# Tail chains in groups of three, and a last pooled attention with its keys in partitions

## The chip, the cores and the metric

The kernel runs on one core of a Trainium2 chip. The metric is device time in microseconds (us) for one execution, the median over runs on the chip.

## What is computed

Four images of 256 channels and 64 x 64 pixels pass through four layers. Each adds the group norm of its input, passed through the layer, to that input.

```python
x = x + layer0(gn(x))   # 1x1 conv, offsets and a gather of 9 points per group, 1x1 convs
x = x + layer1(gn(x))   # qkv (1x1), depthwise 5x5 on qkv, linear attention over both, 1x1 projection
x = x + layer2(gn(x))   # 3x3 conv with binarised weights
x = x + layer3(gn(x))   # pooled attention:
    theta = conv1x1(x); phi, g = conv1x1(maxpool2x2(x))
    m1 = softmax(theta^T phi, over the 1024 pooled keys)     # 4096 queries per image
    m4 = conv1x1(m1 g) + x
```

## The kernel before

All data is float32, with 128 channels on the partitions. The work of an image goes through `convolve` and `offsets`, then `sample` (the gather, `L596`, on GpSimd's queue), `feedforward`, `layer1`, `layer2`, `layer3`. A small planner, `beside`, lays generators side by side: each yields a cost after a piece of work, and is advanced in proportion to a share of the whole. While image n is gathered, the layers of images n-1 and n-2 are written in between. Inside `ordered()` the order of the program is the order of every engine's queue (PE, DVE, ACT, POOL); outside it a list scheduler of the compiler orders them. DMAs are issued by SP.

After the last gather three stages are left, and all that the diff touches and that runs differently lies there (`self.alone` is true):

1. *The tail* (`ordered`): `feedforward` of the last image, then its `layer1` beside `layer2` and most of `layer3` of the image before it. The planner is told that `layer1` costs `LAST` units.
2. `layer2` of the last image, beside the rest of that `layer3` (not ordered).
3. `layer3` of the last image, alone (`wide`, not ordered).

In `layer1`, `rows` makes q, k, v in blocks of 512 pixels and writes them with borders into `pad` tiles of 16 rows (`room(3)` gives four buffers here). 24 *chains* follow: 6 groups of 128 channels x 4 pieces of 16 rows, each a depthwise 5x5, that is 25 products and sums. `aggregate` does a chain on DVE with 25 instructions (the first `L180`, the others `L178`) that accumulate in PSUM (`agg`). `products` does one on ACT, which makes 25 products `m` (`L196`, `L198`), and POOL, which adds 24 of them (`L200`). Here 9 (`ASIDE`) of the 24 are done by `products`: the generator `others` takes the next chain whenever it has finished one, and `step` advances it by 0.67 pieces per DVE instruction through `due`.

What uses the results (transposes and copies `kt` for the sums over pixels, then `output`: `dens`, reciprocal, heads, projection) is put into a list `later` in small stages, and `step` takes one entry for every second DVE instruction. What is left in the list when the last chain has ended is run after it; this is called the drain below.

`layer2` loads each block with a border into `xp` (two buffers here), normalises it on ACT (`L1053`), makes four sums and differences `xd` on POOL (`L1041`), and multiplies (`L1090`).

`layer3` handles 128 queries at a time, 32 times per image, with queries on the partitions: two score matmuls of 512 keys (`L1190`, with the strided slice `tv[:, q]` of `th` as weights), two maxima (`L1191`), `Exp` with the maximum as bias (`L1196`), eight transposes by PE (`L1202`) with two copies `pT` (`L1204`), eight matmuls with `gt` (`L1208`), whose last column of ones gives the softmax's sum, a reciprocal and a scaling `m2` (`L1211`, `L1213`). After each four, a projection (`L1218`), the residual (`L1219`, `L1220`) and a store. For the last image the scores lie in turn in the banks `acc` and `dp` and in the two banks of `agg`. PSUM has eight banks: three `mm`, one `vk`, two `agg`, and `acc` and `dp`.

Of the kernel before, what the change touches and what calls it, by code (L numbers as in the profile page):

```python
# [38 lines left out]

CONVOLVE, OFFSETS, BINARY = NB * 9 + 26, 60, 62  # L40
FEED = NB * 40 + 8
LINEAR, LAST, ASIDE = 938, 592, 9
STEPS = 900
CONV, SECOND = NB * 22.5 + 11, 568
EPS_BN = 1e-5
# [26 lines left out]
class Net:  # L72
# [14 lines left out]

    def long(self):

        return self.ps1.tile([P, 512], F32, name="ps", tag=next(self.idle)) if self.alone else self.ps()  # L90

    def rsqrt(self, pool, v, eps, cols, name):

# [464 lines left out]
    def sample(self, n, ssum):  # L558
# [8 lines left out]
        def halves(name):  # L567

            t = self.ps1.tile([P, 2, 256], F32, name=name, tag=name)
            return cycle([t[:, 0], t[:, 1]])  # L570

        accs, dps = halves("acc"), halves("dp")

        def load(b):
            blocks[b] = sl = sp.tile([P, BR, G * 5], F32, name="sl")
# [181 lines left out]
    def layer1(self, n, st, st2):  # L757
# [3 lines left out]
        with tc.tile_pool(name=f"la{n}", bufs=1, side="right") as sp, \  # L761
# [10 lines left out]
            ld = sp.tile([P, 4, 2, 32], F32, name="ld")  # L772
            nc.vector.memset(ld, 0.0)

            later, count, aside, due = [], 0, None, 0
            alone = self.alone
            room = lambda bufs, more=1: bufs + more * alone

            def step(cost, chains=False):


                nonlocal count, due
                count += chains
                if later and (not alone or count % 2 or not chains):
                    later.pop(0)()
                if chains:
                    if count % 8 == 6 if alone else count in LEADS:
                        next(made, None)
                    if aside:
                        due += ASIDE * 28 / (6 * NCH - ASIDE) / 25  # L790
                        while due > 1:
                            next(aside, None)
                            due -= 1
                return cost


# [12 lines left out]
            def rows():  # L809


                for t, tiles in enumerate(((2, 4), (3, 5), (0, 1))):
                    new = lambda c: [self.padded(bp, 1, 20, 2, c, f"pad{i}", bufs=room(3)) for i in range(2)]
                    pads = {0: new(0)}
                    for b in range(NB):
                        c, h = divmod(b, 2)
# [36 lines left out]
            def products(pd, i, name, done, relu=True, **more):  # L853

                out = bp.tile([P, 16, W], F32, name=name, tag="av2", bufs=3)
                yield from self.products(bp, out, pd, self.w5[:, i], 5, 16, W, 0, self.b5[:, i:i + 1], lambda cost: cost)
                end(out, done, relu, **more)
# [149 lines left out]
                    yield step(3)  # L1007
                return args

            def others():  # L1010

                for _ in range(ASIDE):
                    while not (args := next(every)):
                        yield
                    *args, more = args
                    yield from products(*args, **more)

            if alone:
# [13 lines left out]
    def layer2(self, n, st, st3, side="left"):  # L1032
# [3 lines left out]
        with tc.tile_pool(name=f"ca{n}", bufs=1, side=side) as sp, \  # L1036
# [6 lines left out]
            def normed(b):  # L1043

                lo, hi = max(8 * b - 1, 0), min(8 * b + 9, H)
                xp = bp.tile([P, KT, 10, W + 2], F32, name="xp", bufs=1 + self.alone)
                for v in [xp[:, :, :, 0:1], xp[:, :, :, W + 1:]] + [xp[:, :, 0:1, 1:W + 1]] * (b == 0) \
                        + [xp[:, :, 9:10, 1:W + 1]] * (b == NB - 1):
                    nc.vector.memset(v, 0.0)
                for k in range(KT):  # L1050
                    v = xp[:, k, lo - 8 * b + 1:hi - 8 * b + 1, 1:W + 1]
                    nc.sync.dma_start(v, self.x4_d[n][:, k, lo * W:hi * W].rearrange("p (r w) -> p r w", w=W))
                    nc.scalar.activation(v, v, AF.Identity, bias=bi[:, k:k + 1], scale=sc[:, k:k + 1])  # L1053
                d = xp.rearrange("p k r (x d) -> p k r x d", d=2)
                return [d[:, :, :, c // 2:c // 2 + W // 2, c % 2] for c in range(4)]
# [49 lines left out]
    def layer3(self, n, st, wide=False):  # L1105
        nc, tc, a = self.nc, self.tc, self.a
        M = HW // 4
        with tc.tile_pool(name=f"na{n}", bufs=1, side="left") as sp, \
# [66 lines left out]


            tv = th.rearrange("p (n j) -> p j n", j=NT)
            for b in range(NB):
                m2 = bp.tile([P, 512], F32, name="m2")
                for j in range(4):  # L1180
                    if not wide and not self.spare:
                        s = [self.ps("s") for _ in range(2)]
                    elif wide and j % 2:
                        s = self.ps1.tile([P, 2, 512], F32, name="s", tag="agg")
                        s = [s[:, i] for i in range(2)]
                    else:
                        s = [self.ps1.tile([P, 512], F32, name="s", tag=tag) for tag in ("acc", "dp")]
                    mx = bp.tile([P, 3], F32, name="mx3")
                    for i in range(2):
                        nc.tensor.matmul(s[i], tv[:, 4 * b + j], ph[:, i * 512:(i + 1) * 512], start=True, stop=True)  # L1190
# [32 lines left out]
    def run(self):  # L1223
# [40 lines left out]
        with self.tc.tile_pool(name="gather", bufs=2, side="left") as self.gp, \  # L1264
# [124 lines left out]
```

## Time and profile before

| | us |
|---|---|
| median of 3 runs | 8705.34 (8691.91 to 8707.14) |
| profiled execution | 8769.03 |
| its span | 8767.3 |
| last gather's end, about | 7290 |
| `feedforward` of the last image, about | 7300 to 7520 |
| chains of the last `layer1` on DVE | 7551.6 to 8254.1 |
| drain of their uses | 8254.1 to 8358 |
| last `layer2`, first matmul to last store, about | 8380 to 8560 |
| last `layer3`, its queries' loop | 8590.4 to 8763.4 |

The profile is one execution, taken by the hardware. A group of instructions is given with its line, engine, operation, tiles, count, busy time and mean ns, then the idle time of the engine before them and what ended it. PE is the matmul engine, PEld its weight loads, which overlap with matmuls; a float32 matmul is two instructions. PEclk is the matmul clock that was granted, as a share of full speed.

### The profile page before, as it was taken

Reading aid. Unit: us, or ns where it says so; the run is one execution under the profiler, and the core shown is the slowest. Engines: PE = TensorE matmul, PEld = TensorE weight load, DVE = VectorE, ACT = ScalarE, POOL = GpSimd, SP = SyncE. Lnnn points to the kernel's source line nnn. Section 1 sums busy time; section 2 is a strip of 40 time slices with the busy share of each in tenths; the row PEclk is TensorE's granted clock in tenths of the full one; section 3 lists DMA queues with packets and bytes.
Section 4 is the critical chain, followed back from the end, with each engine's and each line's share of the span. In section 5 each row is a group of like instructions: output and inputs, shape, how many; then the busy total and the mean of one; then the engine's idle time right before and its main releaser. Section 6 shows DMA issues by size and latency. Waiting matters only on the chain.

```text
span 8767.3 us, 99783 instructions
## 1 busy us (share of the span) xinstructions
PE 5927.3 (68%) x35776; PEld 3524.6 (40%) x35776; DVE 4790.2 (55%) x6020; ACT 3564.8 (41%) x10792; POOL 4995.0 (57%) x4894
## 2 busy tenths in 40 slices
PE   4454554448744546688876676888766768987899
PEld 2222222223322322335644443345544433664476
DVE  5344442443366667324776675127766762588723
ACT  2333333234433433344444443444444442456414
POOL 2666666556666666666665556666655560487410
PEclk7666666669866667799987787999878879987899
DMA  6454554454433334444443344444433342220131
GB/s 171 129 157 123 144 150 117 119 146 142 153 107 108 105 109 125 135 130 141 135 133 106 110 115 141 141 133 139 139 105 109 111 118 95 77 68 30 44 96 53
DMA packets 744383, 1031.75 MB, mean 118 GB/s; under 512 B 354128, under 2 KB 459984, under 8 KB 742352
## 3 DMA queue, kind: packets, MB, share of 16 engines
q0 software_dynamic: 221184, 604.27, 24.1%
q1 hardware_dynamic: 522704, 421.10, 16.3%
q8 instruction: 283, 4.64, 0.2%
q14 instruction: 212, 1.74, 0.1%
HBM read 856.39 MB, written 168.61 MB: 117 GB/s over the span
## 4 chain that ended last, share of the span: by engine, by line
PE 42%; another core or an unknown queue 18%; DVE 16%; ACT 13%; issue 8%; POOL 2%; DMA 1%; SPq 0%; ACTq 0%; DVEq 0%; POOLq 0%
DVE agg L178 9%; PE acc L603 6%; PE ps L739 5%; ACT wm L588 5%; PE ps L1090 5%; PE ps L749 5%; PE ps L824 3%; PE ps L946 2%; PE ps L1208 2%; PE s L1190 2%; PE po L636 2%; ACT dT L623 2%; ACT at L608 1%; POOL av L200 1%
## 5 line engine op out<-in xcount | busy, mean ns | idle before, releaser
L596 POOL DMA_INDIRECT g<-tab,sl x4608 | 4401.8, 955 | 2848.3 <-issue 1184.1
L178 DVE SCALAR_TENSOR_TENSOR agg<-pad,vec,agg 128x1024 f32<-128x1024 f32 x2257 | 2904.0, 1287 | 63.3
L603 PE MATMUL acc<-g,wm 128*32 128x128 f32 x18432 | 1018.1, 339 | 2033.0 <-ACT at L608 1573.1
L603 PEld LDWEIGHTS acc<-g,wm 128*32 128x32 f32 x18432 | 562.9, 130 | 2532.2 <-ACT at L608 1785.6
L588 ACT ACTIVATE wm<-sl,con 128x48 f32<-128x48 f32 x6144 | 1486.9, 364 | 25.5 <-remote 12.0
L1090 PE MATMUL ps<-xd,w 128*128 128x256 f32 x3072 | 745.9, 395 | 28.6 <-issue 19.1
L623 ACT COPY dT<-dp 64x128 f32<-64x128 f32 x1152 | 296.3, 257 | 972.9 <-remote 475.5
L1090 PEld LDWEIGHTS ps<-xd,w 128*128 128x128 f32 x3072 | 594.4, 199 | 144.4 <-issue 61.1
L608 ACT COPY at<-acc 128x256 f32<-128x256 f32 x576 | 214.4, 372 | 774.5 <-remote 670.6
L739 PE MATMUL ps<-x2f,f 128*128 128x512 f32 x1024 | 506.6, 643 | 11.8 <-DVE hm L724 7.7
L824 PE MATMUL ps<-xr,qw 128*128 128x512 f32 x768 | 469.2, 741 | 19.5 <-issue 7.4
L724 DVE SCALAR_TENSOR_TENSOR hm<-ps,vec,lk 128x512 f32<-128x512 f32 x256 | 190.6, 749 | 518.7 <-ACT lk L741 391.6
L749 PE MATMUL ps<-hm,f 128*128 128x512 f32 x1024 | 463.5, 601 | 0.0
L200 POOL TENSOR_TENSOR av<-av,m 128x1024 f32<-128x1024 f32 x144 | 342.9, 2382 | 110.8 <-ACT m L196 102.0
L741 ACT ACTIVATE lk<-ps,low 128x512 f32<-128x512 f32 x256 | 174.3, 687 | 529.2 <-PE ps L739 401.5
L1041 POOL TENSOR_TENSOR xd<-xp 128x640 f32<-128x640 f32 x64 | 79.5, 1270 | 522.7 <-ACT xp L1053 421.9
L878 ACT COPY kt<-pt 128x512 f32<-128x512 f32 x256 | 149.2, 583 | 532.5 <-remote 255.6
L636 PE MATMUL po<-dT,ow 128*128 128x288 f32 x1024 | 328.7, 468 | 49.5 <-issue 14.1
L1208 PE MATMUL ps<-gt,pT 128*128 128x129 f32 x2048 | 316.8, 316 | 44.2 <-ACT pT L1204 34.8
L613 PE MATMUL dp<-ident,at 128*128 128x128 f32 x1152 | 288.2, 340 | 83.0 <-ACT dT L623 55.6
L1208 PEld LDWEIGHTS ps<-gt,pT 128*128 128x128 f32 x2048 | 299.1, 227 | 96.4 <-ACT pT L1204 45.8
L1190 PE MATMUL s<-ph,th 128*128 128x512 f32 x512 | 287.6, 673 | 46.0 <-ACT pad L836 12.6
(243 smaller groups left out, 7700.2 us busy)
## 6 DMA issues: line engine op xcount, KB each, us to landing
g<-tab,sl POOLq DMA_INDIRECT x4608
x<-x SPq DMA_DIRECT2D x128, 512.0 KB
xr<-x SPq DMA_DIRECT2D x96, 512.0 KB
tab<-xo SPq DMA_DIRECT2D x192, 128.0 KB
x<-in_x SPq DMA_DIRECT2D x32, 512.0 KB
y<-yc SPq DMA_DIRECT2D x32, 512.0 KB
yb<-y SPq DMA_DIRECT2D x64, 256.0 KB
x<-yb SPq DMA_DIRECT2D x64, 256.0 KB
```

The source lines that it names most:

```text
L178: nc.vector.scalar_tensor_tensor(to, s, wt, acc, ALU.mult, ALU.add)
L588: nc.scalar.activation(wm[:, :, :, o], blocks[b][:, r:r + WR, G:], AF.Copy, scale=self.con("own")[:, o:o + 1])
L596: nc.gpsimd.indirect_dma_start(out=g[:, i, :], out_offset=None, in_=table, in_offset=bass.IndirectOffsetOnAxis(ap=sl.bitcast(I32)[:, r, i: ...
L603: nc.tensor.matmul(acc[32 * i:32 * i + 32, :], wm[:, r4, 4 * i + 2 * x:4 * i + 2 * x + 2, :], g[:, i, x * P:(x + 1) * P], start=x == 0, st ...
L623: nc.scalar.copy(dT[b][hs, :, r:r + UR], dp[u][hs, :, :, s, :].rearrange("p v g o -> p g v o"))
L636: nc.tensor.matmul(po[m][:, 0:BR * OB], self.ow[:, k, m * P:(m + 1) * P], dT[b][:, k].rearrange("p r o -> p (r o)"), start=k == 0, stop=k ...
L739: nc.tensor.matmul(ps, f1[:, k, m * P:(m + 1) * P], x2[:, k], start=k == 0, stop=k == KT - 1)
L749: nc.tensor.matmul(ps, f2[:, k, m * P:(m + 1) * P], hm[:, k], start=k == 0, stop=k == 4 * KT - 1)
L824: nc.tensor.matmul(ps, qw[:, k, m * P:(m + 1) * P], x[:, k], start=k == 0, stop=k == KT - 1)
L1090: nc.tensor.matmul(ps[:, e], w[:, k, t, 2 * half + e, m * P:(m + 1) * P], v[:, 2 * half + e, k, t:t + 8], start=i % 6 == 0, stop=i % 6 == 5)
L1190: nc.tensor.matmul(s[i], tv[:, 4 * b + j], ph[:, i * 512:(i + 1) * 512], start=True, stop=True)
L1208: nc.tensor.matmul(ps[:, 0:P + 1], pT[:, m], gt[:, m], start=m == 0, stop=m == 7)
```

## The change

*Chains.* `ASIDE`, `others` and `due` go. Chains are taken in groups of three: the first and third on DVE, the second on ACT and POOL beside them, a piece for every second DVE instruction; what is left of the second is written at the group's end. So 8 chains are done by `products` and 16 by `aggregate`. `LAST` becomes 624. The second `pad` tile gets one more buffer, `xp` one fewer.

*PSUM.* The banks `acc` and `dp` become one tile `pair` of two banks, in `sample` and after it.

*Last `layer3`.* A new function `turned` makes the scores with keys on the partitions: eight matmuls of 128 keys x 128 queries, `ph` as weights and `tv[:, q]` as the moving operand. The maximum over the keys is taken in two steps, over the eight tiles in PSUM by DVE (with a step of 128 elements) and, after a transpose, over the partitions. To have it along the free axis, ACT spreads it over a 128x128 tile, PE multiplies that with the identity, ACT copies it to SBUF. DVE subtracts it from all 1024 scores of a partition; ACT takes `Exp` of all 1024 at once; the result is already in the form that the matmuls with `gt` need.

```diff
-LINEAR, LAST, ASIDE = 938, 592, 9
+LINEAR, LAST = 938, 624
...
-        return self.ps1.tile([P, 512], F32, name="ps", tag=next(self.idle)) if self.alone else self.ps()
+        return self.pair[:, next(self.idle)] if self.alone else self.ps()
...
-        accs, dps = halves("acc"), halves("dp")
+        pair = self.ps1.tile([P, 2, 2, 256], F32, name="pair", tag="pair")
+        accs, dps = (cycle([pair[:, i, 0], pair[:, i, 1]]) for i in range(2))
...
-                    if aside:
-                        due += ASIDE * 28 / (6 * NCH - ASIDE) / 25
-                        while due > 1:
-                            next(aside, None)
-                            due -= 1
+                    if count % 2 and aside:
+                        next(aside, None)
...
-                    new = lambda c: [self.padded(bp, 1, 20, 2, c, f"pad{i}", bufs=room(3)) for i in range(2)]
+                    new = lambda c: [self.padded(bp, 1, 20, 2, c, f"pad{i}", bufs=room(3) + (alone and i)) for i in range(2)]
...
-            def others():
-
-                for _ in range(ASIDE):
-                    while not (args := next(every)):
-                        yield
-                    *args, more = args
-                    yield from products(*args, **more)
-
-            if alone:
-                aside, number = others(), ASIDE
             while number < 6 * NCH:
                 count = 0 if not alone and number % 2 == 0 else count
                 *args, more = yield from chain()
-                yield from aggregate(*args, **more)
-                number += 1
-            if aside:
-                for _ in aside:
-                    pass
+                if alone:
+
+                    *slow, smore = yield from chain()
+                    aside = products(*slow, **smore)
+                    yield from aggregate(*args, **more)
+                    *args, more = yield from chain()
+                    yield from aggregate(*args, **more)
+                    for _ in aside:
+                        pass
+                    number += 3
+                else:
+                    yield from aggregate(*args, **more)
+                    number += 1
...
-                xp = bp.tile([P, KT, 10, W + 2], F32, name="xp", bufs=1 + self.alone)
+                xp = bp.tile([P, KT, 10, W + 2], F32, name="xp", bufs=1)
...
+            def turned(q, out):
+
+
+                if q % 2:
+                    s = self.ps1.tile([P, 8, P], F32, name="s", tag="agg")
+                else:
+                    s = self.pair.rearrange("p b (m q) -> p (b m) q", q=P)
+                for m in range(8):
+                    nc.tensor.matmul(s[:, m], ph[:, m * P:(m + 1) * P], tv[:, q], start=True, stop=True)
+                mk = bp.tile([P, P], F32, name="mk")
+                nc.vector.tensor_reduce(mk, s.rearrange("p m q -> p q m"), AX.X, ALU.max)
+                ps = self.ps()
+                nc.tensor.transpose(ps[:, 0:P], mk, self.ident)
+                mq = bp.tile([P, 1], F32, name="mq")
+                nc.vector.tensor_reduce(mq, ps[:, 0:P], AX.X, ALU.max)
+                mb = bp.tile([P, P], F32, name="mb")
+                nc.scalar.activation(mb, self.ones, AF.Copy, scale=mq)
+                nc.tensor.matmul(ps[:, P:2 * P], mb, self.ident, start=True, stop=True)
+                mr = bp.tile([P, P], F32, name="mr")
+                nc.scalar.copy(mr, ps[:, P:2 * P])
+                e = bp.tile([P, 8, P], F32, name="e", tag="pe")
+                nc.vector.tensor_tensor(e, s, mr.unsqueeze(1).to_broadcast([P, 8, P]), ALU.subtract)
+                nc.scalar.activation(e, e, AF.Exp)
+                pa = self.ps()
+                for m in range(8):
+                    nc.tensor.matmul(pa[:, 0:P + 1], e[:, m], gt[:, m], start=m == 0, stop=m == 7)
+                rden = bp.tile([P, 1], F32, name="rden")
+                nc.vector.reciprocal(rden, pa[:, P:P + 1])
+                nc.scalar.activation(out, pa[:, 0:P], AF.Copy, scale=rden)
...
+                    if wide:
+                        turned(4 * b + j, m2[:, j * P:(j + 1) * P])
+                        yield 9.5
+                        continue
+                    s = [self.pair[:, i] if self.spare else self.ps("s") for i in range(2)]
...
-        self.idle, self.alone, self.spare = cycle(["acc", "dp"]), True, True
+        self.pair = self.ps1.tile([P, 2, 512], F32, name="pair", tag="pair")
+        self.idle, self.alone, self.spare = cycle([0, 1]), True, True
```

More of the change, by code (lines that the diff above doesn't have):

```diff
@@ L565, in sample @@
         blocks, images, at, dp, dT, po, later = {}, {}, {}, {}, {}, {}, {}
-        def halves(name):
-            t = self.ps1.tile([P, 2, 256], F32, name=name, tag=name)
-            return cycle([t[:, 0], t[:, 1]])
-        accs, dps = halves("acc"), halves("dp")
+        pair = self.ps1.tile([P, 2, 2, 256], F32, name="pair", tag="pair")
+        accs, dps = (cycle([pair[:, i, 0], pair[:, i, 1]]) for i in range(2))
         def load(b):
@@ L773, in layer1 @@
             nc.vector.memset(ld, 0.0)
-            later, count, aside, due = [], 0, None, 0
+            later, count, aside = [], 0, None
             alone = self.alone
@@ L779, in step @@
             def step(cost, chains=False):
-                nonlocal count, due
+                nonlocal count
                 count += chains
@@ L1180, in layer3 @@
                 for j in range(4):
[L1181 to L1187, printed above, removed]
+                    if wide:
[3 more added lines that the diff above has]
+                    s = [self.pair[:, i] if self.spare else self.ps("s") for i in range(2)]
                     mx = bp.tile([P, 3], F32, name="mx3")
```

## The prediction

> **What bounds the kernel now.** I read the page first: the busy time of each engine and the forty slices.
>
> ```profile
> PE 5927.3 (68%) x35776; PEld 3524.6 (40%) x35776; DVE 4790.2 (55%) x6020; ACT 3564.8 (41%) x10792; POOL 4995.0 (57%) x4894
> ...
> PE   4454554448744546688876676888766768987899
> ...
> ```
>
> The whole-span shares say little, because the diff touches only what comes after the last gather, at 7290 us of 8767. So I asked for busy times by stretch: the tail's chains (first to last depthwise instruction on DVE), the drain of their uses, and the last pooled attention from its first score matmul to its last.
>
> ```profile
> 7551.60:8254.10 702.50, 563.45 (x2319) 391.00 (x2318) 630.62 (x714) 437.68 (x596) 545.53 (x242) 0.86 0.17 51
> 8254.10:8358.00 103.90, 92.97 (x321) 50.50 (x320) 42.96 (x68) 30.51 (x50) 0.00 (x0) 0.89 0.16 54
> ...
> 8590.40:8754.70 164.30, 159.15 (x886) 122.78 (x886) 64.79 (x139) 92.31 (x170) 0.00 (x0) 1.00 0.13 46
> ```
>
> The columns are length, then PE, PEld, DVE, ACT, POOL, the granted clock. Chains: DVE works 630.6 of 702.5 us, so DVE bounds them. Drain: PE works 93 of 104. Pooled attention: PE works 159.2 of 164.3, 97%, at full clock, and DVE and ACT have room. Next, the groups and DVE's waits in the chain stretch.
>
> ```profile
> L178 DVE SCALAR_TENSOR_TENSOR agg<-pad,vec,agg 128x1024 f32<-128x1024 f32 x345 | 443.3, 1285 | 8.3
> L200 POOL TENSOR_TENSOR av<-av,m 128x1024 f32<-128x1024 f32 x144 | 342.9, 2382 | 110.8 <-ACT m L196 102.0
> L196 ACT ACTIVATE m<-pad,vec 128x1024 f32<-128x1024 f32 x216 | 246.6, 1158 | 63.0 <-POOL av L200 43.7 <-POOL ak L200 19.0
> ```
>
> ```profile
> DVE rden L1211 <- PE ps L1208: 10.7, 5, 4.9
> ...
> DVE pad L459 <- ACT m L196: 9.2, 1, 9.2
> DVE r L1220 <- PE ps L1218: 4.2, 4, 1.9
> ...
> DVE g_mv L117 <- POOL av L200: 2.0, 1, 2.0
> ```
>
> Last, the groups of the pooled loop.
>
> ```profile
> L1190 PE MATMUL s<-ph,th 128*128 128x512 f32 x128 | 68.9, 638 | 4.2 <-DVE mx L1191 4.2
> L1208 PE MATMUL ps<-gt,pT 128*128 128x129 f32 x512 | 63.4, 276 | 0.5 <-ACT pT L1204 0.5
> L1208 PEld LDWEIGHTS ps<-gt,pT 128*128 128x128 f32 x512 | 61.8, 191 | 8.6 <-issue 4.3 <-ACT pT L1204 1.8
> L1191 DVE TENSOR_REDUCE mx<-s 128x1 f32<-128x512 f32 x64 | 44.3, 691 | 60.0 <-PE s L1190 59.6
> ...
> L1190 PEld LDWEIGHTS s<-ph,th 128*128 128x128 f32 x128 | 34.3, 303 | 12.7 <-DVE mx L1191 8.2 <-issue 0.5 <-ACT ph L1165 0.2
> ```
>
> A weight load of the strided `tv` takes 303 ns where one of packed `pT`, also 128x128, takes 191. This matters below.
>
> **The tail's chains.** Before, 9 of 24 chains run on ACT and POOL, 15 on DVE; after, 8 and 16. So DVE gets 25 more instructions. Five of them in a row took 6.58 us in the timeline, 1.315 us each: +33 us on the engine that bounds. POOL loses 24 adds of 2.38 us (57 us) and ACT 25 products of 1.16 us (29 us); neither bounds, so that by itself gives nothing. What it can give is less waiting on DVE. DVE's waits in the stretch, without the 15.3 us before its first chain, sum to 60 us. Two have a cause that the change takes away: the 9.2 us where the memset of a new `pad1` waits for a chain on ACT to finish with its buffer (`pad1` gets a fifth buffer and no such chain is behind any more), and the 2.0 us behind POOL. The waits behind PE (10.7 and 4.2 us shown) and 3.7 us behind ACT's `ph` could shrink if ACT waits less for POOL (63 us now): at most 18.6 us more. So the tail lies between 33-9.2-2.0-18.6 = +3 and, with nothing given back and a little lost, +38.
>
> The little is `xp` with one buffer. In the timeline an `xp` load is issued within 0.05 us of the end of POOL's adds on the block two before; with one buffer it will follow the adds of the block just before. The adds for block b+1 stand in the last quarter of block b; a block lasts some 35 us; the load takes 4 to 5 us (issue at 8383.66, ACT starts on it at 8387.48 and 8388.72); ACT's use stands an eighth of a block into the next. That is about even: 0 to 2 us a time on ACT, and `m`, `v` and `kt` are queued behind it, then POOL and PE. Seven blocks: 0 to 5 us for DVE, whose idle waits cover part. SP's queue holds the `xr` loads behind a waiting `xp`; these have a second buffer. In the last convolution a block takes 20.7 us against load 5, ACT 2 and POOL 5, so nothing there.
>
> The order of uses: counting the deferred uses through the code, 38 are left when the last chain ends before, 34 after; the `dens` and reciprocal (4.0 us of DVE) of the third output move ahead of that end, and some 5 us of PE leave the drain. Against that, linear's steps now sum to 613 of the 624 given, so about one query of the previous image's attention runs alone after it, 5 us of PE beside the last store. These cancel: drain 0, between -6 and +6. `pair` in place of `acc` and `dp` is the same two banks with the same readers: 0. For the tail I take +20, halfway, since the two waits with a named cause, 11 us, are all I can point at.
>
> **The last pooled attention.** Per query before: 164.3/32 = 5.13 us. PE after: scores 16 instructions of 128 columns, at the pace of L1208 (16 in 1.79 us in the chain) 1.8 us in place of 1.93; eight transposes (0.87 us) go and one (0.11) and a broadcast matmul (0.22) come; output matmuls 1.8 and projection 0.45 stay. That is 4.4 us against 5.05: if PE still bounded, -0.7 us each.
>
> But the path through one score buffer gets longer, and there are two buffers. Before, a buffer was free after scores, two maxima and `Exp`, and its next links needed no buffer. After, it is held for: scores 1.8; maximum over 1024 (0.69 for 512 plus 512 more at the same pace) 1.22; transpose with its load 0.45; maximum over 128 (as L1166) 0.29; `mb` (as L148) 0.40; broadcast matmul 0.5; `mr` (as L1213) 0.35; subtraction of 1024 (as L178) 1.29. Sum 6.3, with eight handoffs of about 0.1, 7.1 us. Two buffers give 3.55 us a query if no link ever waits for its engine. But each engine runs in order, and the other query is half a turn away: the small maximum stands behind a subtraction (1.29), the subtraction behind a maximum (1.22), `mb` behind an `Exp` of 1024 (1.05 as L861 to 1.24 as L198; 1.2), the broadcast behind the output matmuls (1.8). If each link loses that, 7.1+5.5 = 12.6 us a turn, 6.3 a query; if half, 4.9. I laid the instructions out in written order with these durations, each engine taking the earliest written one that is ready, and the two turns locked with the links behind the long ones; so I take the full loss.
>
> The other unknown is the scores' new moving operand, `tv[:, q]`, read with a step of 128 bytes. No matmul of the trace streams such a step; the nearest row is the weight load of the same tile, 112 ns longer than the packed one. Lower bound: no cost (1.8 us). Upper: the same 0.11 us on each of 16 instructions, 3.5 us. I take the upper, as it is the same data through the same engine. The turn is then 14.3 us, 7.15 a query, and PE's own work 6.1. [...] The maximum's read of PSUM with a step of 512 bytes is bounded likewise: 1.22 as above (the nearest, L274 with a step of 1 KB in SBUF, takes 1.04 us for 768) to 1.9 (L529, 288 elements written with gaps, 0.69 against 0.45); I take 1.22.
>
> Sum: 32 x (7.15-5.13) = +65, and the last query's drain is some 3 us longer: +68. With PE busy 85% of the time the clock may fall: 0.89 was granted in the drain at 89% busy, which would add 0.35 us a query, 11 us. Its gaps were up to 5 us and these would be about 1, so I take none and keep 11 for the range.
>
> The profiled execution took 8769.0 us around its span of 8767.3, 0.7% over the median of 8705.3; the differences are small, and I put them on the median unscaled: 8705+20+68 = 8793.
>
> **Rivals.**
> 1. *The step costs PE nothing, the turns still lock*: 32 x (6.3-5.13)+3 = +40, with the tail +20: 8765. [...] Against: the weight load.
> 2. *PE stays the bound* (the other side). In the pooled loop, if the links lose under 1.7 us a turn, PE's work without gaps, 4.4 us, sets the pace: 32 x (4.4-5.13)+3 = -20; with the tail at +3, 8688, and 8682 with the drain at its low end; I price it at 8685. It decides where a turn is under 8.8 us. For it: DVE needs 3.3 and ACT 2.7 us a query, both under 4.4. Against: 7.1 us of links alone.
> 3. *The change does nothing*: the tail's freed waits equal its extra chain and the pooled loop lands at 5.1: 8705.
>
> **How the numbers follow.** A measurement of this kernel tells about 0.2%, 17 us, from no change. Forecast 0.60, rival 1 0.21, rival 2 0.11, rival 3 0.08. The forecast and rival 1 are slower: 0.81; rival 2 faster 0.11; 0.08 same. The low end is rival 1 with the links losing most but not all of 5.5 us (5.5 a query, +15) and the tail at +15: 8735, taken down to 8718 to come near rival 3; rival 2 and most of rival 3, under 2 in 10, stay out. The high end is the forecast with the tail at +38, the clock's 11 and the slower maximum (0.68 a turn, 11): 8835.
>
> **What would show it.** DVE's depthwise instructions after the last gather 400 in place of 375, and the chain stretch some 20 us longer; POOL's idle up, its adds 192; no wait of `pad` for `m`. In the pooled loop PE busy about 85% instead of 97%, waits of the `mr` and subtraction links in front, score matmuls about 0.2 us apart. I am wrong if the loop's PE stays over 95%, or if the score instructions come 0.11 us apart, or if DVE's stretch does not grow.

## The result, and the profile after

The kernel after takes 8941.55 us (median of 5 runs, 8936.2 to 8957.21) against 8707.14 before (8691.91 to 8712.71): the ratio is 1.0272 with a 95% interval of 1.0260 to 1.0284, that is +234 us. The forecast was +88.

I cut both profiles at four points that can be found in any variant: the last matmul of the last `feedforward`, the end of the last depthwise instruction on DVE, the first matmul of the last `layer2`, and the first score matmul of the last `layer3`. Busy times by these stretches, for after (length, then PE, PEld, DVE, ACT, POOL with instruction counts, the granted clock, the DMA share and GB/s):

```profile
7462.10:8272.70 810.60, 606.24 (x2393) 395.11 (x2394) 669.58 (x794) 420.39 (x589) 495.28 (x224) 0.85 0.17 52
8272.70:8390.50 117.80, 101.03 (x362) 58.03 (x362) 43.10 (x87) 37.47 (x61) 1.74 (x2) 0.92 0.26 85
8390.50:8660.80 270.30, 220.40 (x940) 176.23 (x939) 64.41 (x151) 32.82 (x51) 37.79 (x31) 0.94 0.23 66
8660.80:8955.40 294.60, 233.19 (x1154) 208.18 (x1152) 98.92 (x145) 75.48 (x144) 0.00 (x0) 0.83 0.08 27
```

The same four stretches of before lasted 731.0, 126.0, 210.3 and 177.0 us. So three of them grew, by 80, 60 and 118 us, and the drain shrank by 8. The forecast had 20, 0, 68 and 0. DVE works 83% of the first stretch (669.6 of 810.6), and PE 79% of the last, with a clock of 0.83 where it had 1.00. (After's profiled run took 8957.2 us, 16 over its median. Before's was 62 over its median, but that lies ahead of the first cut, which came at 7523.0 against 7462.1 us. So the 249 us between the stretches' sums, less after's 16, agree with the 234 between the medians.)

What DVE waited for in the first stretch of after (total, times, longest), to be held against the waits in the prediction:

```profile
DVE mx L1210 <- PE pair L1209: 46.7, 31, 2.2
DVE x L1061 <- PE pair L1081: 26.2, 7, 17.2
DVE x L1063 <- PE pair L1081: 17.8, 10, 3.2
```

The wait of a `pad` for a chain on ACT is gone, as forecast, but three waits on matmuls into `pair` stand in its place; together they were under 25 us before. The groups of the last pooled loop:

```profile
L1195 PE MATMUL ps<-gt,e 128*128 128x129 f32 x512 | 87.7, 345 | 6.2 <-ACT e L1192 6.2
L1178 PE MATMUL pair<-th,ph 128*128 128x128 f32 x256 | 63.1, 404 | 22.5 <-DVE e L1191 22.5
L1178 PE MATMUL s<-th,ph 128*128 128x128 f32 x256 | 62.1, 398 | 14.7 <-DVE e L1191 14.7
```

A score instruction takes 400 ns. An output matmul of the same size, whose time was 276 ns before, takes 345 at the granted clock of 0.83, and 275 again at 0.99 in run 9 below. PE waits for the subtraction (`L1191`, 37.2 us in all), the last link that holds a score buffer.

### The profile page after: what moved, and what is told of

It reads as the page before. It is cut to its first block, busy times and chain, and to the rows that moved or that the text cites. A ratio compares the mean times of both kernels' runs of the same rounds, so it can differ in the third digit from the quotient of the medians.

```text
span 8955.4 us, 99876 instructions
## 1 busy us (share of the span) xinstructions
PE 5986.4 (67%) x36000; PEld 3572.7 (40%) x36000; DVE 4850.1 (54%) x6045; ACT 3529.3 (39%) x10735; POOL 4938.3 (55%) x4870
## 4 chain that ended last, share of the span: by engine, by line
PE 40%; DVE 14%; ACT 10%; another core or an unknown queue 9%; issue 5%; DMA 0%; POOL 0%; SPq 0%; DVEq 0%; ACTq 0%; POOLq 0%
DVE agg L178 8%; PE ps L735 5%; PE pair L599 5%; PE ps L745 5%; PE ps L817 3%; PE ps L1081 3%; PE pair L1081 3%; ACT wm L584 3%; PE ps L939 3%; PE ps L1227 2%; PE po L632 1%; ACT dT L619 1%; PE s L1209 1%; PE rden L930 1%
## 5 line engine op out<-in xcount | busy, mean ns | idle before, releaser
L178 DVE SCALAR_TENSOR_TENSOR agg<-pad,vec,agg 128x1024 f32<-128x1024 f32 x2280 | 2934.5, 1287 | 63.9
L599 PE MATMUL pair<-g,wm 128*32 128x128 f32 x18432 | 1006.8, 338 | 2019.6 <-ACT at L604 1513.0
L599 PEld LDWEIGHTS pair<-g,wm 128*32 128x32 f32 x18432 | 556.7, 129 | 2518.0 <-ACT at L604 1725.3
L584 ACT ACTIVATE wm<-sl,con 128x48 f32<-128x48 f32 x6144 | 1489.4, 366 | 29.8 <-remote 16.4
L619 ACT COPY dT<-pair 64x128 f32<-64x128 f32 x1152 | 298.0, 259 | 1579.1 <-remote 980.9
L1081 PE MATMUL pair<-xd,w 128*128 128x256 f32 x1536 | 370.9, 392 | 69.0 <-DVE x L1065 45.3
L1081 PE MATMUL ps<-xd,w 128*128 128x256 f32 x1536 | 386.7, 400 | 22.9 <-issue 21.9
L609 PE MATMUL pair<-ident,at 128*128 128x128 f32 x1152 | 287.3, 339 | 112.7 <-ACT dT L619 66.5
L1081 PEld LDWEIGHTS pair<-xd,w 128*128 128x128 f32 x1536 | 291.7, 196 | 137.0 <-DVE x L1065 55.1
L1081 PEld LDWEIGHTS ps<-xd,w 128*128 128x128 f32 x1536 | 297.6, 200 | 93.3 <-issue 56.1
L200 POOL TENSOR_TENSOR ak<-ak,m 128x1024 f32<-128x1024 f32 x96 | 227.8, 2373 | 157.6 <-ACT m L196 153.5
L604 ACT COPY at<-pair 128x256 f32<-128x256 f32 x576 | 214.5, 372 | 226.9 <-remote 165.6
```

Of the source, the lines that this page charges most:

```text
L178: nc.vector.scalar_tensor_tensor(to, s, wt, acc, ALU.mult, ALU.add)
L200: nc.gpsimd.tensor_tensor(acc, acc, made[t - 1], ALU.add)
L584: nc.scalar.activation(wm[:, :, :, o], blocks[b][:, r:r + WR, G:], AF.Copy, scale=self.con("own")[:, o:o + 1])
L599: nc.tensor.matmul(acc[32 * i:32 * i + 32, :], wm[:, r4, 4 * i + 2 * x:4 * i + 2 * x + 2, :], g[:, i, x * P:(x + 1) * P], start=x == 0, st ...
L609: nc.tensor.transpose(dp[u][:, v].rearrange("p g s o -> p (g s o)"), at[u][:, v], self.ident)
L619: nc.scalar.copy(dT[b][hs, :, r:r + UR], dp[u][hs, :, :, s, :].rearrange("p v g o -> p g v o"))
```

## The experiments

The runs below were made on four other chips: 1 to 4 on the first, 5 to 8 on the second, 9 to 11 on the third, 12 and 13 on the fourth. The kernel before took 7735 us on the first of these and 8765 to 8778 us on the others. That difference lies ahead of the first cut: the feed-forward ended at 6488 us in the third run below and at 7523 us in before's profile, and the first three stretches of that run, whose code there is before's, lasted 731.5, 126.0 and 210.4 us against before's 731.0, 126.0 and 210.3. So ratios are taken against before on the same chip, and stretches are compared across chips. One profile's first stretch is good to about 12 us: eight kernels with the same code there (runs 1 and 4 to 10) took 726 to 738.

| kernel | chains | drain | last `layer2` | last `layer3` | sum | ratio to before (95%) |
|---|---|---|---|---|---|---|
| before | 731.0 | 126.0 | 210.3 | 177.0 | 1244.3 | |
| after | 810.6 | 117.8 | 270.3 | 294.6 | 1493.3 | 1.0272 (1.0260 to 1.0284) |
| 1 chains alone | 730.0 | 106.5 | 214.8 | 177.0 | 1228.3 | 0.9981 (0.9972 to 0.9990) |
| 2 `pair` alone | 791.0 | 133.8 | 254.2 | 179.8 | 1358.8 | 1.0146 (1.0130 to 1.0161) |
| 3 turned scores alone | 731.5 | 126.0 | 210.4 | 295.2 | 1363.1 | 1.0153 (1.0139 to 1.0166) |
| 4 after on two tiles | 729.9 | 106.5 | 211.2 | 294.6 | 1342.2 | 1.0132 (1.0117 to 1.0148) |
| 5 packed theta | 729.8 | 109.0 | 210.8 | 238.3 | 1287.9 | 1.0042 (1.0026 to 1.0059) |
| 6 no maximum | 738.3 | 110.8 | 209.5 | 192.4 | 1250.9 | 1.0001 (0.9988 to 1.0013) |
| 7 no maximum, packed | 726.7 | 109.0 | 211.1 | 144.8 | 1191.6 | 0.9935 (0.9912 to 0.9958) |
| 8 written order, packed | 726.4 | 105.7 | 213.6 | 164.8 | 1210.4 | 0.9960 (0.9947 to 0.9973) |
| 9 written order, step kept | 738.2 | 110.8 | 209.5 | 205.3 | 1263.8 | 1.0016 (1.0006 to 1.0026) |
| 10 `pair` in last `layer2` alone | 737.6 | 110.8 | 255.6 | 296.0 | 1400.0 | 1.0175 (1.0154 to 1.0197) |
| 11 `pair`, one `xp` | 790.7 | 133.8 | 256.6 | 179.8 | 1360.9 | 1.0135 (1.0119 to 1.0152) |
| 12 chains and `pair` | 803.4 | 117.9 | 265.1 | 179.8 | 1366.3 | 1.0146 (1.0124 to 1.0169) |
| 13 after again | 809.8 | 117.9 | 266.8 | 294.6 | 1489.1 | 1.0262 (1.0241 to 1.0283) |

### 1. The chains alone

Of the diff only the groups of three, `LAST`, the fifth `pad` buffer and `bufs=1` of `xp` are made.

> The kernel before with the groups of three, their staged uses, the pads and the one buffer of xp, but with acc and dp as two tiles and the old pooled loop. Theory A (the one tile pair makes PE and DVE take turns, in the tail and in the last convolution): the chains alone cost what was forecast, +15 to +35 us, so 8722 to 8742 us; the stretch from the feed-forward's end to the last chain takes about 755 us against 731 before, the last convolution 210 us as before, and DVE waits on PE at the groups' sums for under 15 us. Theory B (the order of the chains and the single buffer of xp did it): +80 in the stretch and +62 in the convolution, less 11 at the drain, so about 8838 us.

Measured: 0.9981, 15 us *faster*. Rival B is out, but so is theory A's number. The first two stretches of the kernel with before's chains (run 3), and then of this one:

```profile
6488.00:7219.50 731.50, 583.56 (x2385) 405.49 (x2384) 639.23 (x766) 447.84 (x613) 552.77 (x248) 0.86 0.19 57
7219.50:7345.50 126.00, 108.83 (x384) 62.47 (x383) 48.73 (x95) 42.21 (x68) 1.33 (x2) 0.86 0.28 89
```

```profile
6490.30:7220.30 730.00, 575.59 (x2394) 397.74 (x2395) 666.14 (x794) 419.54 (x589) 494.72 (x224) 0.88 0.19 58
7220.30:7326.80 106.50, 95.32 (x365) 55.08 (x364) 43.80 (x88) 37.14 (x60) 1.78 (x2) 0.96 0.28 95
```

DVE's extra chain is there (+26.9 us busy, 28 more instructions) and all of it went into DVE's idle time, which fell from 92.3 to 63.9 us. In the drain PE's busy time fell by 13.5 us, although at full clock it would be nearly the same work (108.83 x 0.86 = 93.6 against 95.32 x 0.96 = 91.5): by this estimate the clock is what changed, and PE's idle time fell from 17.2 to 11.2.

### 2. `pair` alone

```diff
-        accs, dps = halves("acc"), halves("dp")
+        pair = self.ps1.tile([P, 2, 2, 256], F32, name="pair", tag="pair")
+        accs, dps = (cycle([pair[:, i, 0], pair[:, i, 1]]) for i in range(2))
...
-                        s = [self.ps1.tile([P, 512], F32, name="s", tag=tag) for tag in ("acc", "dp")]
+                        s = [self.pair[:, i] for i in range(2)]
```

> The kernel before with acc and dp made one tile of two banks, pair, used by the sampling, the linear attention's sums and projections, the last convolution and the old pooled loop; the chains, the pads, xp's two buffers and the old softmax stay. Theory A: +40 to +60 us in the tail and about +62 us in the last convolution, so 8807 to 8830 us, with PE waiting there for DVE some 80 us; the old pooled loop, whose two halves now share a tile, may lose up to 1 us a query more (+16 for the 16 even queries). Theory B: within 15 us of 8705.

Measured: 1.0146, +115 us between medians: 60 in the chain stretch, 8 in the drain, 44 in the last `layer2`, 3 in the last loop. Theory A holds in the sum (+102 to +125), but its 62 us for the last `layer2` came out as 44. (The sampling has `pair` too, and there it costs nothing that can be seen: the last `feedforward` ended at 6491.7 us here and at 6488.0 in run 3.) PE's waits in this kernel's chain stretch:

```profile
PE pair L1186 <- DVE mx L1187: 48.8, 22, 7.8
PE pair L1086 <- DVE x L1070: 18.0, 13, 2.4
...
PE pair L1086 <- DVE x L1066: 12.1, 14, 2.4
```

`L1186` is the score matmul of the image before, which in this stretch writes the first half of `pair`, has its maximum taken, and writes the second half. With two tiles the second matmul ran beside the first maximum: in run 3's chain stretch no score matmul waits for one. Here it waits for a read of the half that it does not write. This is the largest piece of what I had priced at nothing.

### 3. The turned scores alone

`acc` and `dp` get a pool of their own, which ends before the last loop; then a pool with `pair` opens.

> The kernel before with the turned scores alone: acc and dp stay two tiles to the end of the last convolution, and only then a tile of two banks takes their place. Theory A: all of the 118 us lost in the last pooled loop is the turned loop's own: 8825 us (8815 to 8835), 8.5 us a query, TensorE's clock near 0.84 there. Theory B (part of it comes from what pair did earlier in the kernel): the forecast's +68, 8773 us, 7.15 us a query.

Measured: 1.0153, +119 us, all of it in the last loop (295.2 against 177.0). Theory A holds: the whole price of the loop is its own.

### 4. After, on two tiles until the last loop

Runs 1 and 3 joined.

> The kernel after, but with acc and dp as two tiles until the last convolution has ended; the one tile of two banks comes only then, for the turned scores. Chains, staged uses, xp's one buffer and the turned scores are those of after. Theory A: after less 62 in the convolution and less 45 to 60 in the tail: 8818 to 8840 us, and the sum of the differences of the chains alone and of the pooled part alone holds within 10 us. Theory B: within 15 us of after, 8941.

Measured: 1.0132, +103 us; the parts give -15+119 = 104. So these two add up (theory A's range began at +113, as it put the chains at +15 or more), and the last `layer2` is back at 211 us with one `xp` buffer. This kernel is the base of runs 5 to 10.

### 5 to 7. What sets the pace of the turned loop

Run 5 stores theta so that a query's operand is contiguous:

```diff
-            th = sp.tile([P, HW], F32, name="th")
+            th = sp.tile([P, NT, P], F32, name="th")
...
-                nc.scalar.activation(th[:, b * 512:(b + 1) * 512], ps, AF.Identity, bias=tb)
+                nc.scalar.activation(th[:, :, 16 * b:16 * b + 16].rearrange("p j n -> p n j"), ps.rearrange("p (n j) -> p n j", j=NT), AF.Identity, bias=tb)
...
-            tv = th.rearrange("p (n j) -> p j n", j=NT)
+            tv = th
```

> The kernel with two tiles acc and dp, the new chains and the turned scores, with one edit: theta is stored with the pixels of a query group side by side, so the score matmuls read their moving operand without the 128-byte step; the activation that stores theta writes with a step instead. Theory A (the step doubles the stream, and the turn of a score buffer with the order of the queue sets the pace): score instructions 0.11 to 0.12 us apart against 0.21 to 0.24; a turn loses some 1.8 to 3.6 us for two queries, so the last pooled loop takes 237 to 266 us against 294.6. Theory B (the maximum across partitions sets it, and the stream lies beside it): 285 to 295 us. Theory C (TensorE's own work is all that counts): 1.8 us times 32 queries less, about 237 us or under.

Run 6 removes everything from `mk` to `mr`, and:

```diff
-                nc.vector.tensor_tensor(e, s, mr.unsqueeze(1).to_broadcast([P, 8, P]), ALU.subtract)
-                nc.scalar.activation(e, e, AF.Exp)
+                nc.scalar.activation(e, s, AF.Exp)
```

> The same base with the turned scores, without the maximum: no reduction over the keys, no transposition, no second reduction, no broadcast and no subtraction; Exp reads the scores from PSUM. It leaves out the subtraction of the maximum. The strided moving operand stays. Theory A: the chain of the maximum holds the score buffers; without it TensorE is the bound at 3.5 + 2.0 us a query and the last pooled loop takes 190 to 210 us against 294.6. Theory B (the strided stream and the clock set the pace): 265 to 280 us, since only 0.6 us of TensorE's work a query goes.

Run 7 is both.

> Both edits together: packed theta and no maximum (it leaves out the subtraction of the maximum). Each query has only its scores (1.8 us), Exp and the output matmuls (2.0 us) left. All theories: 3.8 to 4.2 us a query and 20 us of ends, so 140 to 155 us in the last pooled loop; the difference to the run without the maximum but with the step is the whole price of the step where TensorE is the bound: 45 to 58 us.

Measured: 238.3, 192.4 and 144.8 us in the loop, against 294.6. The step costs 56.3 us with the maximum and 47.6 without it; the maximum's links cost 102.2 with the step and 93.5 without. Theory B of run 5 and theory B of run 6 fall. Run 5 lies where its theories A and C meet, so it does not say whether the 93.5 us are the links themselves or the order in which PE takes them. Run 8 does.

### 8 and 9. The order written out

In after, the last loop is ordered by the compiler's list scheduler. Here is what that order does to one query (timeline of after, all engines, start and length):

```profile
8670.56 3.76 PE L1178 MATMUL pair<-th,ph 128*128 128x128 f32 x16 [0.84 <-DVE e L1191]
...
8671.52 0.39 ACT L1186 ACTIVATE mb<-ones,mq 128x128 f32<-128x128 f32 x1
8674.14 2.35 PE L1195 MATMUL ps<-gt,e 128*128 128x129 f32 x16
...
8676.33 0.39 PE L1187 MATMUL ps<-ident,mb 128*128 128x128 f32 x2
...
8677.29 1.23 DVE L1191 TENSOR_TENSOR e<-s,mr 128x1024 f32<-128x1024 f32 x1 [0.59 <-ACT mr L1189]
...
8678.66 2.42 PE L1178 MATMUL s<-th,ph 128*128 128x128 f32 x10 [1.94 <-DVE e L1191]
```

The second query's `mb` is ready at 8671.91, but the broadcast (`L1187`) that reads it stands in PE's queue behind 16 score instructions of the next query and 16 output instructions of the one before, and starts at 8676.33, 4.4 us late. The buffer `s` comes free that much later, and PE then waits 1.94 us for it.

So long a wait of the broadcast is not the rule: over 3 us in 9 of the 32 queries, 2.0 in 4, at most 0.35 in 19, and 1.6 on average. The commoner loss lies one link earlier, at the transposition (`L1182`). From PE's timeline of after:

```profile
8701.77 0.39 PE L1187 MATMUL ps<-ident,mb 128*128 128x128 f32 x2
8703.86 2.44 PE L1178 MATMUL pair<-th,ph 128*128 128x128 f32 x10 [1.70 <-DVE e L1191]
8706.13 3.38 PE L1195 MATMUL ps<-gt,e 128*128 128x129 f32 x16
8709.34 0.27 PE L1182 MATMUL ps<-ident,mk 128*128 128x128 f32 x1
8709.45 1.48 PE L1178 MATMUL pair<-th,ph 128*128 128x128 f32 x6
```

The `mk` of the query in `s` was ready at 8701.48, but its transposition stands behind a broadcast, 10 score instructions that themselves wait for a buffer, and 16 output instructions, and starts at 8709.34, 7.9 us late. The other query's scores, 16 instructions, are split into 10 and 6 around those output matmuls and take 7.1 us. Averaged over the 30 queries whose buffer is written again, by the start and end times in after's trace, the transposition waits 3.55 us and a query's scores last 6.15 us from first to last.

Run 8 has packed theta and this order, by hand, over three queries (`lowered`: broadcast, `mr`, subtraction, `Exp`; `most` and `wide_most`: the two maxima and `mb`; `left`: the projection):

```diff
+                for k in range(NT + 3):
+                    if k < NT:
+                        scores(k, 0, 4)
+                    if 0 <= k - 1 < NT:
+                        lowered(k - 1)
+                    if k < NT:
+                        scores(k, 4, 8)
+                    if 0 <= k - 2 < NT:
+                        values(k - 2)
+                    if k < NT:
+                        most(k)
+                    if 0 <= k - 2 < NT:
+                        divided(k - 2)
+                    if k < NT:
+                        wide_most(k)
+                    if k >= 3 and (k - 3) % 4 == 3:
+                        left((k - 3) // 4)
```

> The same base with packed theta and the maximum kept, but the last loop's order written out over three queries: the scores of query k, the broadcast and the subtraction of k-1, the output matmuls of k-2. Theory A (the queue's order lengthens the turn: a query's transposition and broadcast stand behind another's 16 score or 16 output instructions): TensorE's own 4.4 to 4.6 us a query is the bound again, so the last pooled loop takes 160 to 180 us, near the 177 of the kernel before. Theory B (the links' own latencies make the turn, whatever the order): 230 to 265 us, as with packed theta alone.

Run 9 is the same with `th` stored as in after.

> The written-out order of the last loop as in the run before, with the maximum kept, but theta again stored so that a query's pixels lie 128 bytes apart. Theory A (the step is TensorE's own work, 1.5 to 1.76 us a query as the two pairs of runs so far gave, and with the order written out TensorE is the bound): 164.8 + 32 x 1.5 to 1.76 = 213 to 221 us in the last pooled loop. Theory B (in the written order the step hides in the waits of the chain): under 195 us.

Measured: 164.8 and 205.3 us. The last stretch of runs 5, 8 and 9:

```profile
8581.40:8819.70 238.30, 174.76 (x1154) 153.66 (x1152) 99.18 (x145) 75.17 (x144) 0.00 (x0) 0.90 0.10 34
```

```profile
8575.20:8740.00 164.80, 152.72 (x1154) 133.97 (x1152) 101.51 (x146) 79.76 (x146) 0.00 (x0) 1.00 0.14 49
```

```profile
8577.00:8782.30 205.30, 195.58 (x1154) 179.55 (x1152) 102.65 (x145) 77.55 (x146) 0.00 (x0) 0.99 0.11 39
```

The instructions are the same 1154 matmul instructions each time. The written order alone takes 73.5 us off (238.3 to 164.8) and brings the clock to 1.00. PE is then the bound, busy 152.7 of 164.8 us. A query takes 4.65 us (148.9 us from first to last score, for 32), and 4.44 where no projection lies between. By the same averages the transposition now waits 0.05 us (2.55 in run 5), and a query's scores last 2.35 us (4.29 in run 5). From PE's timeline of run 8:

```profile
8630.30 1.06 PE L1187 MATMUL pair<-th,ph 128*128 128x128 f32 x8
8631.34 0.49 PE L1202 MATMUL ps<-ident,mb 128*128 128x128 f32 x2
8631.67 1.06 PE L1187 MATMUL pair<-th,ph 128*128 128x128 f32 x8
8632.56 1.95 PE L1212 MATMUL ps<-gt,e 128*128 128x129 f32 x16
8634.58 0.33 PE L1193 MATMUL ps<-ident,mk 128*128 128x128 f32 x1
8634.74 1.06 PE L1187 MATMUL s<-th,ph 128*128 128x128 f32 x8
```

Theory A of run 8 holds. Run 9 fell between its two theories: the step costs 40.5 us, 1.27 us a query and not 1.5 to 1.76, though each score instruction is 120 ns longer (395 against 275). Counted from the start of each instruction on PE to the next one's, the scores of a query take 3.58 us against 2.00, but the output matmuls, the transposition and the broadcast around them take 2.27 against 2.56, 0.29 less.

Run 8 is the fastest kernel here that keeps the maximum: 0.9960, 35 us under before.

### 10 and 11. `pair` in the last `layer2`

Run 10 is run 4, but `acc` and `dp` end before the last `layer2`, so that this runs on the halves of `pair`.

> The kernel with two tiles acc and dp, the new chains and the turned scores, with one edit: acc and dp end before the last convolution, which then runs on the two halves of one tile of two banks. Theory A (a read of one half is ordered between the writes of the other, because the order is kept for the whole tile): the convolution takes 254 to 270 us against 211, TensorE waits there for DVE's reads about once in each of the 32 halves, the chain stretch stays at 730 and the pooled loop at 295. Theory B (what happened in the tail set the convolution's pace in after, through the clock or through late transfers): 211 to 216 us.

Measured: 255.6 us against 211.2, and the other stretches as in run 4, within the 12 us. Theory A holds. PE waited 27 times for a read of `pair` in this stretch, 36 us in all, where it has no such wait in run 4:

```profile
PE pair L1090 <- DVE x L1074: 26.0, 14, 2.9
...
PE pair L1090 <- DVE x L1070: 10.2, 13, 0.8
```

PE's timeline of after, and DVE's between, show the pattern:

```profile
8446.57 5.45 PE L1081 MATMUL pair<-xd,w 128*128 128x256 f32 x24 [1.57 <-DVE x L1065]
8452.80 5.45 PE L1081 MATMUL pair<-xd,w 128*128 128x256 f32 x24 [0.78 <-DVE x L1061]
8461.08 5.45 PE L1081 MATMUL pair<-xd,w 128*128 128x256 f32 x24 [2.83 <-DVE x L1065]
```

```profile
8445.04 0.69 DVE L1063 TENSOR_TENSOR x<-x,pair 128x512 f32<-128x512 f32 x1 [1.88 <-PE pair L1081]
8445.76 0.42 DVE L1064 TENSOR_TENSOR x<-x,pair 128x256 f32<-128x256 f32 x1
8446.10 0.42 DVE L1065 TENSOR_TENSOR x<-x,pair 128x256 f32<-128x256 f32 x1
```

A half takes 24 instructions. The read of a finished half is written after 9 of the next half's 12 matmuls. With one tile, the next matmul, into a half that nobody reads, waits for the end of that read (0.78 us for the single read, 1.57 and more for three), and the read had waited for the matmuls before it. PE and DVE take turns after every 24 instructions.

Run 11 is run 2 with `bufs=1` for `xp`.

> The kernel before with the one tile pair everywhere (old chains, old pooled loop) and, besides, xp with one buffer. It asks for the 31 us by which after exceeds the sum of the parts (16 us in the convolution: 270.3 against 210.3 + 44 from pair + 1 to 5 from the single xp). Theory A (the single xp and pair lengthen each other, since a block's last products are held up and with them the next image's loading): the convolution takes 265 to 270 us, against 254.2 with two buffers of xp, the chain stretch stays near 791. Theory B (it is the new chains' order that does it): 254 to 259 us in the convolution.

Measured: 256.6 us, so theory B: the single `xp` buffer adds 2.4 us to `pair`, no more.

### 12 and 13. Do the parts add up?

Run 12 is runs 1 and 2 joined; run 13 is after itself.

> The kernel before with the new chains, xp's one buffer and the one tile pair, but the old pooled loop. By medians the parts alone made -15 (chains), +115 (pair) and +119 us (turned scores), 219 in all, and after made +234. Theory A (the parts add up): +100 us (90 to 110), a chain stretch near 790 and a convolution near 255. Theory B (the new chains and pair lengthen each other): +115 to +135 us, a chain stretch of 805 to 815 and a convolution near 270, as the profiled run of after shows them.

> After itself, beside the run above on one chip, with another profiled execution. Theory A: +219 us over the kernel before (205 to 230), and this profile's stages sum to less than the first's 1493.3 us after the feed-forward. Theory B: +230 to +250, with the stages of the first profile within 5 us.

Measured: 1.0146 (+109 to +148 us by its interval) and 1.0262 (+212 to +248). The four stretches of run 12 are 122.0 us over before's, where runs 1 and 2 give -16.0+114.5 = 98.5. So chains and `pair` together cost some 24 us more than each alone, half of it in the chain stretch (803.4); the medians are hardly fine enough to show it. For run 12 theory B is the nearer one (803.4 and 265.1 us, +118 between the medians). Run 13 does not decide: +224 between its medians lies in theory A's range, and its stretches sum to 1489.1, within the 5 us that theory B asked for. In the last `layer2`, 5.6 of the 8.5 us between runs 12 and 11 are one wait of PE for an `Exp` of the image before, whose attention ends beside it; run 11 has no such wait. But why the extra chain is no longer absorbed once `pair` is there was not tried, and stays open.

## Why the prediction was wrong, point by point

The direction was right, the size was not: +88 forecast, +234 measured, of which `pair` is 115, the turned loop 119, the chains -15, and the rest, 15, what chains and `pair` cost together beyond this (24 by the stretches of run 12).

**"`pair` in place of `acc` and `dp` is the same two banks with the same readers: 0."** This step failed most. The banks and readers are the same, but with one tile PE waited for reads of the half that it did not write (27 times, 36 us, in run 10's last `layer2`, and never in run 4's). I had priced the edit by what it moves, which is nothing, and not by which instructions it now orders one behind another. Runs 2 and 10 show the price: 60+8+44+3 us. Before's trace held the warning. In its chain stretch PE waited once for a read of `acc` or `dp`:

```profile
PE ps L1090 <- DVE x L1074: 3.0, 1, 3.0
```

So the overlap that the edit forbids was in use; in run 2 the three waits shown above sum to 79 us.

**The tail's chains, +20 within +3 to +38.** The sign failed: the stretch did not grow (730.0 us in run 1 against 731.0), and with the drain the chains alone brought -15. The 25 extra instructions were there (400 depthwise instructions on DVE, 192 adds on POOL), and the given-back term was mis-sized: 28.4 us of DVE's idle time went, where I took 13 of a possible 29.8. That limit had left out DVE's waits behind PE for `x` and `mx`, 24.0 us before. Apart from the 9.2 us at the `pad`, the first chain's wait for its first `pad` went from 15.6 to 8.1 us, which I had left out, and the three largest waits behind PE (for `rden`, `x` and `mx`) fell from 30.6 us in run 3 to 14.2 in run 1. Against these stands one new wait at the single `xp`, 6.2 us of DVE for POOL. **"Drain 0"** failed too: -20. I counted uses and forgot that PE bounds the drain (busy 108.8 of 126.0 us in run 3) at a clock below full (0.86); in run 1 less idle time (11.2 us against 17.2) and a faster clock (0.96) came together; no run here parts the two. The 0 for a single `xp` in the last `layer2` was near: +4.5, +0.9 and +2.4 us in runs 1, 4 and 11.

**The last pooled loop, 7.15 us a query.** Measured 8.5 from first to last score (271 us for 32) and +118 in all. Of its terms, the step of `tv` was taken at its upper bound, 1.8 us, and it cost 1.27 (runs 8 and 9) to 1.76 (after and run 5); rival 1 is out. The runs show 395 ns against 275 for each score instruction (run 9 against run 8). The maximum over PSUM with a step of 512 bytes took 1.22 us, as taken.

What failed is the sum for a buffer's turn, 14.3 us for two queries, against 17.2 on average in after. It charged 5.5 us for four links that wait for their engine, and these waited 2.5 (the broadcast 1.5 of the 1.8). What it left at nothing cost more. The transposition was charged no wait and stood 3.55 us behind other queries' work on PE. The scores were charged as 3.5 us in one piece and lasted 6.15, split by output matmuls and at a clock of 0.84. A free buffer was written again after 0.74 us. These are 6.9 us left out; that the sum was only 2.9 short is luck, since the charged waits, links and handoffs were 4.0 too long. I had let every engine take the earliest written instruction that is ready; the order that ran was another.

The clock term failed too. I took it as 0 and kept 11 us for the range, because the gaps would be short; it was 0.83, with no gap over 2.45 us between the scores. No run shows that short gaps leave the clock at full speed; before's drain, at 0.89, had none over 3.18 us, where I had written 5. With the same 1154 instructions PE was busy 233.2 us in after and 195.6 in run 9, whose clock was 0.99. From run 9 to after the loop loses 89 us to the order and the clock that came with it, 38 as PE's longer busy time and 52 as idle time. The full account of +118: the step 40, the order and its clock 89, and -12 that the turned scores bring when both are mended (164.8 against 177.0).

**Rival 2** (PE stays the bound at 4.4 us a query) is nearly what the written order made true: 4.65 with the projections, and -12 us in the loop where it had -20. It was right about the engines and wrong about the order that would run. For the kernel as it stood it is out.

**What would show it.** Right: the counts on DVE and POOL, no wait of `pad` for `m`, PE near 85% (82% from first to last score, but by luck, as its busy time was longer at the lower clock: 233.2 us against run 9's 195.6), PE's longest waits for the subtraction, score instructions about 0.2 us apart. Wrong: the chain stretch 20 us longer (80 in after, none with the chains alone).

## What to carry to other kernels

Two buffers that two engines use in turn should stay two tiles: joining them costs nothing in memory, and here it took the overlap away (+115 us in run 2), so price such an edit by listing who writes one half while the other is read. The longer chain of links between engines paid here only with a queue order made for it (164.8 us against 238.3 without it and 177.0 before); lay out the order over several iterations, each link placed where its input is just ready, before judging the algorithm by its time. And where PE is near to bounding a stretch, look at the granted clock beside its idle gaps: this loop, against the written order of run 9, had 52 us more of idle time, and 38 us of longer busy time besides, at a clock of 0.83 against 0.99.

## What the runs showed of the hardware that I had not expected

The clock fell without long gaps. In the turned loop of after, from first to last score, the trace's clock records show 22 stretches at half clock, 3.4 or 6.8 us each, 85.3 us together, while the longest time that PE stood still was 2.45 us (19 gaps over 1 us; 49 us of gaps in all). Each of the 22 came right after a stretch of 3.4 us in which PE was busy 31 to 74%; of the 32 such stretches there after which the full clock stayed, 29 were 78% busy or more. In run 8, whose loop was granted 1.00, there was none between the first score and the last.

The score matmuls' moving operand, read with a step of 128 bytes, cost PE 120 ns more for each of the two instructions of a 128-column float32 matmul (395 ns in run 9 against 275 in run 8); the same step in a weight load cost 112 ns before (303 against 191).
